# Two more x slots in a three-stage convolution network, with the second stage emitted from a table

## The chip, the cores and the metric

The kernel runs on one core of one Trainium2 chip. The metric is the device time of one execution in microseconds. The engines are TensorE (PE), VectorE (DVE), ScalarE (ACT), GpSimd (POOL), and SyncE (SP), which here only issues transfers. "Turn" means one round of the second stage's loop, one tile.

## The reference

The input x has 8192 samples of 8 channels of 16 by 16 pixels. Four layers follow each other, each of the form `x = x + layer(group_norm(x))`, with four groups of two channels:

```
x = x + tensor_train(gn(x), core0, core1, core2) + bias      # layer 0, a dense map of each sample
x = x + relu(batch_norm(conv3x3(gn(x), w1) + b1))            # layer 1, batch norm over all samples
x = x + conv3x3(quantize(gn(x)), quantize(w2)) + b2          # layer 2, int8 scale from max|gn(x)|
x = x + conv3x3(edge_pad(gn(x)), binarize(w3)) + b3          # layer 3
```

Two of these need the whole batch before they can go on. Batch norm in layer 1 needs the mean and variance over all samples, and layer 2 needs the largest absolute value of the normalised x. They cut the kernel into three stages.

## The kernel before

A tile is 128 samples: 128 partitions (channel and row) by 2048 fp32 numbers (sample and column), 1 MiB. There are 64 tiles. All stages run through them.

**Stage one** computes layer 0 and the convolution of layer 1 in quarters of a tile. It stores each tile's x (`x1_d`) and convolution output y (`y_d`) to DRAM, except those of the last four tiles, which stay in SBUF (`STAY`). A part of each quarter's input goes out to DRAM (`limb_d`) and comes back in another layout by a transfer that POOL issues (`fetch`, 252 of them, the only ones POOL issues[...]). All other large transfers are issued by SP, in order. `conv1_stats` collects mean and variance of each tile in `bnst`. At the end, a short chain over all 64 tiles turns `bnst` into the batch norm's factor and offset, `bn_a` and `bn_b`.

**Stage two** takes the tiles in `order2`, the four that stayed first. For each tile i it does, on the engine in brackets:

- load y and x (`load2`, SP), each into a slot of a ring, `y_slots` (eight) and `x_slots` (`KEEP`, 13);
- relu of y with `bn_a`, `bn_b` (ACT), then x = x + y (POOL; for a few tiles half on DVE, table `SPLIT`);
- the square of x (ACT), sums of x and its square over the groups (PE), reduction and transposition of these (DVE), two small copies (ACT), the variance (DVE), its power of -1/2 (POOL);
- the statistics widened (ACT) and spread to the samples (PE), x minus its mean (`centre2`, DVE; for three late tiles half on POOL), the store of x (SP), and the largest absolute value by sample (`range2`, DVE), combined by four tiles (`top`).

The loop's iteration i handles the add of tile i, the sums of tile i-2 and the centring of tile i-3. `InOrder` keeps the program order of PE, DVE, ACT and POOL, so the order in which the loop emits the steps is the order in which each engine does them. Of the 64 tiles, 13 stay in SBUF for stage three and are not stored (`kept`). The last five (`LATE`) load y and x into y buffers that earlier tiles have left, and are stored.

**Stage three** does layers 2 and 3 and stores the result. Its order is written out as a table of phases (`PHASE`, `PERIOD`), sorted by due time. It begins when the last `amax` is known.

Of the kernel before, what the change touches and what calls it, by code (L numbers as in the profile page):

```python
# [8 lines left out]
F32 = mybir.dt.float32  # L9
# [4 lines left out]
ALU = mybir.AluOpType  # L14
# [4 lines left out]
P = 128  # L19
# [3 lines left out]
G = 4  # L23
# [6 lines left out]
KEEP = 13  # L30
# [23 lines left out]
SPLIT = {0: 0.5, 1: 0.5, 2: 0.5, 3: 0.5, -2: 0.5, -1: 0.5}  # L54
# [9 lines left out]
def tile_net(ctx: ExitStack, tc: tile.TileContext, xb, xt_in, pack0, pack1, pack2, out):  # L64
# [22 lines left out]
    xs, bs, ys, sqs, (xh,) = ([hold.tile([P, F], F32, name=f"{n}{k}") for k in range(m)]  # L87
                            for n, m in (("xs", 4), ("bs", 2), ("ys", 2), ("sq", 2), ("xh", 1)))
# [7 lines left out]
    x_slots = ([xs[t % 4] for t in order2[:STAY]] + [u[:, h * F:(h + 1) * F] for u in us for h in range(2)] + y_stay[:3])  # L96
# [3 lines left out]
    LATE = 5 if NT >= KEEP + STAY + 3 else 0  # L100
# [19 lines left out]
    mhalf = const.tile([P, 64], F32, name="mhalf")  # L120
# [169 lines left out]
    bnst = const.tile([P, NT, 2], F32, name="bnst")  # L290
    gnst = const.tile([P, NT, 2 * G], F32, name="gnst")
# [36 lines left out]
    with first as s:  # L328
# [274 lines left out]
        for n in range(NT * NQ):  # L603
# [59 lines left out]
            if n == NT * NQ - 2 and NT > STAY + 3:  # L663
                load2(STAY)
                load2(STAY + 1)

        t = NT - 1
        if NT > STAY + 3:
            load2(STAY + 2, "x")
            load2(STAY + 3, "x")  # L670
# [5 lines left out]
        if NT > STAY + 3:  # L676
            load2(STAY + 2, "y")
# [6 lines left out]
        for i in ((t - 1, 2), (t - 1, 3), (t, 0), (t, 1), (t, 2), (t, 3)):  # L684
            conv1_stats(*i)

# [3 lines left out]
    with tc.tile_pool(name="bn", bufs=1) as bn, tc.tile_pool(name="bnp", bufs=1, space=PSUM) as bnp:  # L690
        msum = bn.tile([P, 1], F32, name="msum")
        nc.vector.tensor_reduce(msum, bnst[:, :, 0], AX.X, ALU.add)
        mps_ = bnp.tile([P, 1], F32, name="mps_")
        nc.tensor.matmul(mps_, L["avg16"], msum, start=True, stop=True)
        bmean = bn.tile([P, 1], F32, name="bmean")
        nc.vector.tensor_copy(bmean, mps_)
        dev = bn.tile([P, NT], F32, name="dev")
        nc.vector.tensor_scalar(dev, bnst[:, :, 0], bmean, None, ALU.subtract)
        nc.vector.tensor_tensor(dev, dev, dev, ALU.mult)
        nc.vector.tensor_tensor(dev, dev, bnst[:, :, 1], ALU.add)  # L700
        vsum = bn.tile([P, 1], F32, name="vsum")
        nc.vector.tensor_reduce(vsum, dev, AX.X, ALU.add)
        vps = bnp.tile([P, 1], F32, name="vps")
        nc.tensor.matmul(vps, L["avg16"], vsum, start=True, stop=True)
        bvar = bn.tile([P, 1], F32, name="bvar")
        nc.vector.tensor_scalar(bvar, vps, EPS, None, ALU.add)
        nc.gpsimd.tensor_tensor(bvar, bvar, mhalf[:, 0:1], ALU.pow)
        nc.vector.tensor_tensor(bn_a, L["gamma"], bvar, ALU.mult)
        nc.vector.tensor_tensor(bmean, bmean, bn_a, ALU.mult)
        nc.vector.tensor_tensor(bn_b, L["beta"], bmean, ALU.subtract)  # L710
# [14 lines left out]
    def stats_pow(mv):  # L725
        pool.tensor_tensor(mv[:, G:2 * G], mv[:, G:2 * G], mhalf[:, :G], ALU.pow)
# [4 lines left out]
    with tc.tile_pool(name="p2", bufs=2) as p2, tc.tile_pool(name="ps2", bufs=2, space=PSUM) as ps2:  # L731
        T = T2
        x_slots[STAY + 4:STAY + 4] = [more.tile([P, F], F32, name=f"xk{k}") for k in range(2)]
# [24 lines left out]
        def sum2(i):  # L758
            x, y = T[i]["x"], T[i].pop("y")
            y_used[i] = y  # L760
            act.activation(y, y, AF.Relu, bias=bn_b, scale=bn_a)
            n = int(F * SPLIT.get(i if i < NT // 2 else i - NT, 0))
            if n < F:
                pool.tensor_tensor(x[:, n:], x[:, n:], y[:, n:], ALU.add)
            if n:
                dve.tensor_tensor(x[:, :n], x[:, :n], y[:, :n], ALU.add)
# [9 lines left out]
        def stats2(i):  # L776

            st, mv = psc[:, 32 + 32 * (i % 2):64 + 32 * (i % 2)], gnst[:, place[order2[i]]]
            red = small.tile([P, 32], F32, name=f"s_c{i}", tag="s")
            dve.tensor_reduce(red, T[i].pop("ps").rearrange("p (b w) -> p b w", w=4), AX.X, ALU.add)  # L780
            dve.transpose(st, red)
            T[i]["sq"] = small.tile([P, G], F32, name=f"sq_c{i}", tag="sqm")
            act.copy(mv[:, 0:G], st[:, 0:G])
            act.activation(T[i]["sq"], st[:, 0:G], AF.Square)

        def sigma2(i):
            st, mv = psc[:, 32 + 32 * (i % 2):64 + 32 * (i % 2)], gnst[:, place[order2[i]]]
            dve.scalar_tensor_tensor(mv[:, G:2 * G], st[:, G:2 * G], EPS, T[i].pop("sq"), ALU.add, ALU.subtract)
            stats_pow(mv)

        def spread2(i):
            T[i]["gb"] = ps = ps2.tile([P, BANK], F32, name=f"gb_{i}", tag="gb")
            wide = p2.tile([P, 2 * G, P // G], F32, name=f"wide_{i}", tag="wide")
            act.copy(wide, gnst[:, place[order2[i]]].unsqueeze(2).to_broadcast([P, 2 * G, P // G]))
            if i % 4 == 0:
                T[i]["gr"] = ps2.tile([P, 4, P], F32, name=f"gr_{i}", tag="gr")
                T[i]["top"] = p2.tile([P, 4, P], F32, name=f"top_{i}", tag="top")
            else:
                T[i]["gr"], T[i]["top"] = T[i - 1]["gr"], T[i - 1]["top"]
            for k, dst in enumerate((ps[:, 0:P], T[i]["gr"][:, i % 4])):  # L800
                pe.matmul(dst, wide[:, k * G:(k + 1) * G].rearrange("p g n -> p (g n)"), ident, start=True, stop=True)

        def centre2(i):
            x, ps = T[i]["x"], T[i]["gb"]
            engines = [dve, dve]
            if NT - 4 <= i < NT - 1:
                engines, mean = [dve, pool], small.tile([P, P], F32, name=f"gm_{i}", tag="rows")
                a, b = HALVES[1]
                act.copy(mean[:, a:b], ps[:, a:b])
            for engine, (a, b) in zip(engines, HALVES):  # L810
                engine.tensor_tensor(samples(x)[:, a:b], samples(x)[:, a:b], over_w(ps if engine is dve else mean, a, b),
                                     ALU.subtract)
            if NT - KEEP - LATE <= i < NT - LATE:
                kept[order2[i]] = x
            else:
                nc.sync.dma_start(x2_d[order2[i]], x)
# [12 lines left out]
        def on(i, f):
            if 0 <= i < NT:  # L830
                f(i)

        BEGUN = STAY + 3 if NT > STAY + 3 else STAY
        AHEAD2 = len(y_slots) - 1


        free = STAY + AHEAD2 - 1
        for i in [*range(STAY), *range(BEGUN, free)]:
            on(i, lambda i: load2(i, "y" if i == BEGUN > STAY else "yx"))
        y_used = {}  # L840
        late = [(k, j) for j in range(NT - LATE, NT) for k in "yx"]
        for i in range(NT + 4):
            if i == 1:
                on(free, load2)
            if i + AHEAD2 < NT - LATE:
                on(i + AHEAD2, lambda i: i <= free or load2(i))
            elif late:
                k, j = late.pop(0)
                T2[j][k] = y_used[i - 1]
                nc.sync.dma_start(T2[j][k], (x1_d if k == "x" else y_d)[order2[j]])  # L850
            if i == 8:
                operands3()
            on(i, sum2)
            on(i - 2, sums2)
            on(i - 3, spread2)
            on(i - 1, square2)
            on(i - 2, stats2)
            on(i - 3, centre2)
            on(i - 2, sigma2)
            on(i - 3, range2)  # L860
# [20 lines left out]
    with ExitStack() as s:  # L881
# [4 lines left out]
        AHEAD = min(NT, KEEP - 6)  # L886
# [250 lines left out]
```

## Time and profile before

| what | value |
|---|---|
| median of 3 runs | 3813.59 us (3813.19 to 3816.85) |
| profiled execution | 3814.16 us, span 3812.4 us |
| busy share of PE, DVE, ACT, POOL | 94%, 87%, 67%, 79% |
| moved by DMA | 961.45 MB, 252 GB/s over the span |
| first relu of stage two | at 2625.65 us |
| last `top` of stage two | ends at 3059.25 us |

Shares of busy time are means over stages with different limits, so the table alone says little. Times in the text are microseconds from the start of the span. A line of a window table has the stretch, its length, then busy time and number of instructions of PE, PE's weight loads, DVE, ACT and POOL, then the granted clock of PE, the busy share of DMA, and GB/s. A line of the chain or a timeline has start, duration, engine and what is done; a bracket gives the idle time before and what ended it. A line of waits has the sum, the number and the longest.

### The profile page before, as it was taken

To read this page: it belongs to the slowest core of one execution; us is meant where nothing else is said; L and a number is where in the kernel's file an instruction comes from. 1 tells how busy PE (TensorE), PEld (TensorE's weight loads), DVE (VectorE), ACT (ScalarE), POOL (GpSimd) and SP (SyncE) were. 2 spreads that over 40 slices of the span, in tenths; PEclk is the share of its full clock that TensorE was granted. 3 is DMA by queue.
4 is the path that set the end of the run, shared out by engine and by line. 5 is a ranking of instruction groups with operands and counts; after the bars stand their busy time and mean duration, and the time that the engine had idled before them with its cause. 6 is when DMAs were issued, how large, how long until landed. Compare 5 with 4: busy or idle time off the path is not lost.

```text
span 3812.4 us, 60771 instructions
## 1 busy us (share of the span) xinstructions
PE 3585.7 (94%) x20358; PEld 2259.7 (59%) x20422; DVE 3324.4 (87%) x5896; ACT 2544.5 (67%) x2805; POOL 3006.3 (79%) x3100
## 2 busy tenths in 40 slices
PE   8999999999999999999999999997555679999999
PEld 4666666666666666666666666664444546666665
DVE  8988888888888888888888888877977888888887
ACT  5666666666666666666666666665765678888885
POOL 4877777778777777777787777765977769999998
PEclk9999999999999999999999999998866689999999
DMA  5787887887877878878878788766999824444442
GB/s 213 253 268 257 259 269 256 260 264 251 271 254 260 271 254 262 270 254 261 264 251 272 253 260 271 254 193 257 425 425 425 335 89 185 188 179 189 187 166 111
DMA packets 210840, 961.45 MB, mean 252 GB/s; under 512 B 44896, under 2 KB 45152, under 8 KB 110048
## 3 DMA queue, kind: packets, MB, share of 16 engines
q1 hardware_dynamic: 173808, 692.22, 48.9%
q0 software_dynamic: 36288, 264.26, 23.4%
q8 instruction: 163, 2.67, 0.3%
q14 instruction: 149, 1.22, 0.1%
q10 hardware_dynamic: 432, 1.08, 0.1%
HBM read 578.84 MB, written 378.54 MB: 251 GB/s over the span
## 4 chain that ended last, share of the span: by engine, by line
PE 85%; DMA 7%; POOL 4%; DVE 3%; issue 1%; ACT 1%; SPq 0%; DVEq 0%; POOLq 0%
PE po L43 45%; PE pu L43 12%; PE pf L43 10%; PE pm L43 6%; PE pq L43 4%; PE pc L43 3%; PE s L43 3%; DMA yk<-y_d 2%; POOL u L43 1%; DMA x_d<-u 1%; DMA u<-x_d 1%; POOL xs L43 1%; PE ps_a L43 1%; POOL gnst L43 1%; DMA x_d<-xk 1%
## 5 line engine op out<-in xcount | busy, mean ns | idle before, releaser
L43 PE MATMUL po<-u,core 128*128 128x512 f32 (+1 forms) x4112 | 1844.3, 591 | 0.7 <-DVE xs L43 0.7
L43 ACT COPY u<-pu 128x2048 f32<-128x2048 f32 x512 | 956.4, 1868 | 515.7 <-PE pu L43 515.6
L43 PEld LDWEIGHTS po<-u,core 128*128 128x128 f32 x4112 | 744.7, 190 | 737.4 <-issue 735.3
L43 PE MATMUL pu<-core2r,xl 128*128 128x256 f32 x4032 | 678.5, 310 | 4.8 <-ACT u L43 3.4
L43 PEld LDWEIGHTS pu<-core2r,xl 128*128 128x128 f32 x4032 | 527.9, 189 | 128.0 <-issue 123.1
L43 POOL TENSOR_TENSOR bs<-bs,xh 128x512 fp32r<-128x512 f32 (+1 forms) x253 | 325.7, 1288 | 203.6 <-ACT xh L43 201.7
L43 POOL TENSOR_TENSOR v<-e 128x128 f32<-128x128 f32 x750 | 397.3, 541 | 0.0
L43 DVE TENSOR_TENSOR xs<-po,xs 128x512 f32<-128x512 f32 x256 | 176.9, 691 | 220.3 <-PE po L43 220.3
L43 ACT ACTIVATE m<-pm,b 128x128 f32<-128x128 f32 x250 | 91.9, 368 | 394.8 <-PE pm L43 394.7
L43 PEld LDWEIGHTS pm<-v,fast 128*128 128x128 f32 x2000 | 262.5, 191 | 119.7 <-issue 105.9
L43 POOL TENSOR_TENSOR e<-x1n,x 128x512 f32<-128x512 f32 x250 | 305.5, 1222 | 31.3 <-ACT x L43 23.8
L43 DVE TENSOR_TENSOR bs<-bs,stat 128x1024 f32<-128x1024 f32 x252 | 290.5, 1214 | 2.1
L43 POOL TENSOR_TENSOR xs<-xs,w 128x2048 f32<-128x2048 f32 x64 | 291.5, 4555 | 0.7 <-DMA xs<-in_xt 0.7
L43 PE MATMUL pm<-v,fast 128*128 128x128 f32 x2000 | 263.5, 275 | 0.0
L43 ACT ACTIVATE x<-x1n 128x512 f32<-128x512 f32 x500 | 246.9, 544 | 7.6 <-DVE x1n L43 7.6
L43 PE MATMUL pf<-hi,sign 128*128 128x512 f32 x768 | 231.6, 439 | 0.4 <-ACT bs L43 0.4
L43 PE MATMUL pf<-lo,sign 128*128 128x512 f32 x768 | 218.9, 422 | 0.0
L43 POOL TENSOR_TENSOR v<-r 128x128 f32<-128x128 f32 x500 | 215.6, 447 | 0.0
L43 POOL DMA_DIRECT2D xl<-limb_d x252 | 149.8, 595 | 81.2 <-DMA limb_d<-xh 24.1
L43 POOL TENSOR_TENSOR mvb<-mvb,mhalf 128x4 f32<-128x4 f32 x64 | 66.3, 1036 | 172.0 <-DVE mvb L43 165.8
L43 PE MATMUL gb<-ident,wide 128*128 128x128 f32 x128 | 43.2, 433 | 166.6 <-ACT wide L43 166.6
L43 ACT ACTIVATE sq<-xs 128x2048 f32<-128x2048 f32 x103 | 197.4, 1917 | 1.9 <-POOL xs L43 1.7
(323 smaller groups left out, 7307.9 us busy)
## 6 DMA issues: line engine op xcount, KB each, us to landing
xl<-limb_d POOLq DMA_DIRECT2D x252, 1024.0 KB, 7.4
x_d<-xs SPq DMA_DIRECT2D x76, 1024.0 KB, 8.4
xs<-in_xt SPq DMA_DIRECT2D x64, 1024.0 KB, 7.5
bs<-in_xb SPq DMA_DIRECT2D x63, 1024.0 KB, 5.8
limb_d<-xh SPq DMA_DIRECT2D x1008, 64.0 KB, 4.5
limb_d<-bs SPq DMA_DIRECT2D x1008, 64.0 KB, 5.1
y_d<-ys SPq DMA_DIRECT2D x60, 1024.0 KB, 8.1
u<-x_d SPq DMA_DIRECT2D x34, 1024.0 KB, 6.1
```

The costliest lines, as they stand in the source:

```text
L43: return self.tc.keep_in_program_order(op(*args, **kwargs))
```

## The change

Two more x buffers (`ex`) stand in the ring of stage two, so `KEEP` is 15[...]. `LATE` becomes 6. Four x tiles rather than two are loaded around the end of stage one in another order. The batch norm is computed with a shift: the mean of 62 tiles is taken first, the sums of squares about it over 63 tiles are made before the last tile's statistics, and the last tile is added by a second matmul into the same accumulator. The second stage's steps are emitted from a table (`PHASE2`, one turn is `TURN` = 6.0), with changed times for the last five tiles (`SHIFT2`) and changed shares of DVE and POOL for the last tiles (`SPLIT`, `POOL2`). The preparation of stage three's operands (`operands3`) moves from turn 8 to turn 32.

```diff
-KEEP = 13
+KEEP = 15
...
-SPLIT = {0: 0.5, 1: 0.5, 2: 0.5, 3: 0.5, -2: 0.5, -1: 0.5}
+TURN = 6.0
+PHASE2 = {"relu": 0.0, "add": 0.3, "sums": 12.6, "rows": 18.9, "spr": 19.2, "sq": 7.5, "red": 13.8, "cp": 14.1, "cen": 20.4,
+          "store": 20.7, "sig": 15.0, "pow": 15.3, "rng": 21.6, "top": 21.9, "addv": 0.31}
+SHIFT2 = {-5: {"top": 9.4, "relu": -3, "sq": -1.3},
+          -4: {"top": 18.3, "rng": 10.2, "cen": 1.4, "store": 11.7},
+          -3: {"store": 4.0, "sums": -0.3, "cen": 3, "top": 33.8, "rng": 6.4, "sq": -4.0},
+          -2: {"sums": -3.7, "spr": 1.0, "store": 8.4, "relu": -8.6, "rng": 12.1, "sq": -3.0, "top": 46.0, "red": -2.6},
+          -1: {"cp": 0.1, "addv": 2.0, "red": 0.3, "pow": 1.3, "top": 60.5, "rng": 58.5, "store": 39.9, "spr": 10.6,
+            "cen": 16.3, "relu": -4.3, "sq": -1.0}}
+SPLIT = {0: 0.5, 1: 0.5, 2: 0.5, 3: 0.5, -2: 0.25, -1: 0.75, -3: 0.25}
+POOL2 = {-4: 0.5, -3: 0.5, -2: 0.5, -1: 0.5, -5: 0.25}
...
-    x_slots = ([xs[t % 4] for t in order2[:STAY]] + [u[:, h * F:(h + 1) * F] for u in us for h in range(2)] + y_stay[:3])
+    x_slots = ([xs[t % 4] for t in order2[:STAY]] + ex + [u[:, h * F:(h + 1) * F] for u in us for h in range(2)] + y_stay[:3])
-    LATE = 5 if NT >= KEEP + STAY + 3 else 0
+    LATE = 6 if NT >= KEEP + STAY + 3 else 0
...
-            if n == NT * NQ - 2 and NT > STAY + 3:
-                load2(STAY)
-                load2(STAY + 1)
+            for i, k in {NT * NQ - 6: [(0, "x"), (1, "x")], NT * NQ - 2: [(0, "y"), (2, "x"), (1, "y"), (3, "x")]}.get(n, []):
+                load2(STAY + i, k)
...
-            load2(STAY + 2, "x")
-            load2(STAY + 3, "x")
+        dve.tensor_reduce(shift, bnst[:, 0:seen, 0], AX.X, ALU.add)
+        load2(STAY + 4, "x")
+        load2(STAY + 5, "x")
...
-        for i in ((t - 1, 2), (t - 1, 3), (t, 0), (t, 1), (t, 2), (t, 3)):
+        mps = ps_m.tile([P, BANK], F32, name="mps", tag="mm")
+        pe.matmul(mps[:, 0:1], L["avg16"], shift, start=True, stop=True)
+        for i in ((t - 1, 2), (t - 1, 3), (t, 0), (t, 1), (t, 2)):
             conv1_stats(*i)
+        dve.tensor_scalar(shift, mps[:, 0:1], 1.0 * NT / seen, None, ALU.mult)
+        dev = small.tile([P, 2, t], F32, name="dev", tag="turned")
+        dve.tensor_scalar(dev[:, 0], bnst[:, 0:t, 0], shift, None, ALU.subtract)
+        dve.tensor_tensor(dev[:, 1], dev[:, 0], dev[:, 0], ALU.mult)
+        dve.tensor_tensor(dev[:, 1], dev[:, 1], bnst[:, 0:t, 1], ALU.add)
+        dve.tensor_reduce(part, dev, AX.X, ALU.add)
+        conv1_stats(t, 3)
+        dve.tensor_scalar(last[:, 0:1], bnst[:, t, 0:1], shift, None, ALU.subtract)
+        dve.scalar_tensor_tensor(last[:, 1:2], last[:, 0:1], last[:, 0:1], bnst[:, t, 1:2], ALU.mult, ALU.add)
...
+        for k, src in enumerate((part, last)):
+            nc.tensor.matmul(moments, L["avg16"], src, start=(k == 0), stop=(k == 1))
+        nc.vector.tensor_scalar(bvar[:, 1:2], moments[:, 0:1], moments[:, 0:1], None, ALU.mult)
+        nc.vector.scalar_tensor_tensor(bvar[:, 0:1], moments[:, 1:2], EPS, bvar[:, 1:2], ALU.add, ALU.subtract)
+        nc.gpsimd.tensor_tensor(bvar[:, 0:1], bvar[:, 0:1], mhalf[:, 0:1], ALU.pow)
+        nc.vector.tensor_scalar(nmean, moments[:, 0:1], shift, -1.0, ALU.add, ALU.mult)
+        nc.vector.tensor_tensor(bn_a, L["gamma"], bvar[:, 0:1], ALU.mult)
+        nc.vector.scalar_tensor_tensor(bn_b, nmean, bn_a, L["beta"], ALU.mult, ALU.add)
...
+            n = P - int(P * share(POOL2, i))
+            if n < P:
+                mean = small.tile([P, P], F32, name=f"gm_{i}", tag="rows")
+                act.copy(mean[:, n:], ps[:, n:P])
+                pool.tensor_tensor(x[:, n:], x[:, n:], over_w(mean, n, P), ALU.subtract)
...
+        for i, k in [(3, "y"), (6, "x"), (4, "y"), (7, "x"), (5, "y"), (6, "y")]:
+            load2(STAY + i, k)
+        todo2 = [(when(op, i), OPS2[op], (i,)) for i in range(NT) for op in OPS2]
+        todo2 += [(when("relu", i - AHEAD2, -.2), load2, (i, "y")) for i in range(STAY + AHEAD2, NT - LATE)]
+        todo2 += [(when("add", i - TURNX, .6) if i < KEEP else when("relu", i - 8, -.1), load2, (i, "x"))
+                  for i in range(TURNX, NT - LATE)]
+        todo2 += [(when("add", NT - LATE - AHEAD2 - 1 + n, .6), late2, (n,)) for n in range(2 * LATE)]
+        todo2.append((when("relu", NT // 2, -.3), operands3, ()))
...
-        AHEAD = min(NT, KEEP - 6)
+        AHEAD = min(NT, KEEP - 8)
...
-    nc = bacc.Bacc("TRN2", target_bir_lowering=False, num_devices=1)
+    nc = bacc.Bacc("TRN2", target_bir_lowering=False, num_devices=1, dynamic_dma_scratch_size=1536)
```

More of the change, by code (lines that the diff above doesn't have):

```diff
@@ L86, in tile_net @@
     hold = ctx.enter_context(tc.tile_pool(name="hold", bufs=1))
-    xs, bs, ys, sqs, (xh,) = ([hold.tile([P, F], F32, name=f"{n}{k}") for k in range(m)]
-                            for n, m in (("xs", 4), ("bs", 2), ("ys", 2), ("sq", 2), ("xh", 1)))
+    xs, bs, ys, sqs, (xh,), ex = ([hold.tile([P, F], F32, name=f"{n}{k}") for k in range(m)]
+                            for n, m in (("xs", 4), ("bs", 2), ("ys", 2), ("sq", 2), ("xh", 1), ("ex", 2)))
     us = [hold.tile([P, 2 * F], F32, name=f"u{k}") for k in range(2)]
@@ L119, in tile_net @@
     make_identity(nc, ident)
-    mhalf = const.tile([P, 64], F32, name="mhalf")
+    mhalf = const.tile([P, G], F32, name="mhalf")
     pool.memset(mhalf, -0.5)
@@ L290, in tile_net @@
     bnst = const.tile([P, NT, 2], F32, name="bnst")
+    bnw = const.tile([P, 6], F32, name="bnw")
     gnst = const.tile([P, NT, 2 * G], F32, name="gnst")
@@ L662, in tile_net @@
                 conv1(*quarter_of(n, LAG))
-            if n == NT * NQ - 2 and NT > STAY + 3:
-                load2(STAY)
-                load2(STAY + 1)
+            for i, k in {NT * NQ - 6: [(0, "x"), (1, "x")], NT * NQ - 2: [(0, "y"), (2, "x"), (1, "y"), (3, "x")]}.get(n, []):
+                load2(STAY + i, k)
         t = NT - 1
-        if NT > STAY + 3:
-            load2(STAY + 2, "x")
-            load2(STAY + 3, "x")
+        seen = max(1, NT - 2)
+        shift, nmean, part, last = bnw[:, 0:1], bnw[:, 1:2], bnw[:, 2:4], bnw[:, 4:6]
+        dve.tensor_reduce(shift, bnst[:, 0:seen, 0], AX.X, ALU.add)
+        load2(STAY + 4, "x")
+        load2(STAY + 5, "x")
         conv1_output(t - 1, 1)
@@ L675, in tile_net @@
         quarter_apply(t, 2)
-        if NT > STAY + 3:
-            load2(STAY + 2, "y")
+        load2(STAY + 2, "y")
         conv1_direct(t, 1)
@@ L690, in tile_net @@
     with tc.tile_pool(name="bn", bufs=1) as bn, tc.tile_pool(name="bnp", bufs=1, space=PSUM) as bnp:
[L691 to L710, printed above, removed]
+        moments = bnp.tile([P, 2], F32, name="moments")
+        for k, src in enumerate((part, last)):
+            nc.tensor.matmul(moments, L["avg16"], src, start=(k == 0), stop=(k == 1))
+        bvar = bn.tile([P, 2], F32, name="bvar")
+        nc.vector.tensor_scalar(bvar[:, 1:2], moments[:, 0:1], moments[:, 0:1], None, ALU.mult)
[4 more added lines that the diff above has]
+        nc.vector.scalar_tensor_tensor(bn_b, nmean, bn_a, L["beta"], ALU.mult, ALU.add)
     def sums_pe(ps, x, sq):
@@ L732, in tile_net @@
         T = T2
-        x_slots[STAY + 4:STAY + 4] = [more.tile([P, F], F32, name=f"xk{k}") for k in range(2)]
+        x_slots[STAY + 6:STAY + 6] = [more.tile([P, F], F32, name=f"xk{k}") for k in range(2)]
         y_slots += [p2.tile([P, F], F32, name=f"yk{k}", bufs=1) for k in range(4)]
@@ L756, in operands3, with relu2, share, add2 @@
             L["select"]("back2", [3], L["band3"][:, 0])
-        def sum2(i):
-            x, y = T[i]["x"], T[i].pop("y")
-            y_used[i] = y
+        def relu2(i):
+            y = T[i]["y"]
             act.activation(y, y, AF.Relu, bias=bn_b, scale=bn_a)
-            n = int(F * SPLIT.get(i if i < NT // 2 else i - NT, 0))
+        def share(table, i):
+            return table.get(i if i < NT // 2 else i - NT, 0)
+        def add2(i):
+            n = int(F * share(SPLIT, i))
             if n < F:
-                pool.tensor_tensor(x[:, n:], x[:, n:], y[:, n:], ALU.add)
+                pool.tensor_tensor(T[i]["x"][:, n:], T[i]["x"][:, n:], T[i]["y"][:, n:], ALU.add)
+        def addv2(i):
+            n = int(F * share(SPLIT, i))
             if n:
-                dve.tensor_tensor(x[:, :n], x[:, :n], y[:, :n], ALU.add)
+                dve.tensor_tensor(T[i]["x"][:, :n], T[i]["x"][:, :n], T[i]["y"][:, :n], ALU.add)
         def square2(i):
@@ L776, in stats2 @@
         def stats2(i):
-            st, mv = psc[:, 32 + 32 * (i % 2):64 + 32 * (i % 2)], gnst[:, place[order2[i]]]
+            st = psc[:, 32 + 32 * (i % 2):64 + 32 * (i % 2)]
             red = small.tile([P, 32], F32, name=f"s_c{i}", tag="s")
@@ L781, in stats2, with means2 @@
             dve.transpose(st, red)
+        def means2(i):
+            st, mv = psc[:, 32 + 32 * (i % 2):64 + 32 * (i % 2)], gnst[:, place[order2[i]]]
             T[i]["sq"] = small.tile([P, G], F32, name=f"sq_c{i}", tag="sqm")
@@ L788, in sigma2, with power2, wide2 @@
             dve.scalar_tensor_tensor(mv[:, G:2 * G], st[:, G:2 * G], EPS, T[i].pop("sq"), ALU.add, ALU.subtract)
-            stats_pow(mv)
+        def power2(i):
+            stats_pow(gnst[:, place[order2[i]]])
+        def wide2(i):
+            T[i]["wide"] = p2.tile([P, 2 * G, P // G], F32, name=f"wide_{i}", tag="wide")
+            act.copy(T[i]["wide"], gnst[:, place[order2[i]]].unsqueeze(2).to_broadcast([P, 2 * G, P // G]))
         def spread2(i):
+            wide = T[i].pop("wide")
             T[i]["gb"] = ps = ps2.tile([P, BANK], F32, name=f"gb_{i}", tag="gb")
-            wide = p2.tile([P, 2 * G, P // G], F32, name=f"wide_{i}", tag="wide")
-            act.copy(wide, gnst[:, place[order2[i]]].unsqueeze(2).to_broadcast([P, 2 * G, P // G]))
             if i % 4 == 0:
@@ L803, in centre2, with store2 @@
         def centre2(i):
[L804 to L812, printed above, removed]
+            x, ps = samples(T[i]["x"]), T[i]["gb"]
+            n = P - int(P * share(POOL2, i))
[3 more added lines that the diff above has]
+                pool.tensor_tensor(x[:, n:], x[:, n:], over_w(mean, n, P), ALU.subtract)
+            for a in range(0, n, P // 2):
+                b = min(n, a + P // 2)
+                dve.tensor_tensor(x[:, a:b], x[:, a:b], over_w(ps, a, b), ALU.subtract)
+        def store2(i):
             if NT - KEEP - LATE <= i < NT - LATE:
-                kept[order2[i]] = x
+                kept[order2[i]] = T[i]["x"]
             else:
-                nc.sync.dma_start(x2_d[order2[i]], x)
+                nc.sync.dma_start(x2_d[order2[i]], T[i]["x"])
         def range2(i):
@@ L823, in range2, with top2 @@
                                   apply_absolute_value=True)
+        def top2(i):
+            top = T[i]["top"]
             if i % 4 == 3 or i == NT - 2:
@@ L827, in range2 @@
                 dve.tensor_reduce(amax[:, at:at + 1], top[:, a:b].rearrange("p a b -> p (a b)"), AX.X, ALU.max)
[L829 to L860, printed above, removed]
+        def late2(n):
+            k, j = "yx"[n % 2], NT - LATE + n // 2
+            T2[j][k] = T[NT - LATE - AHEAD2 - 1 + n]["y"]
+            nc.sync.dma_start(T2[j][k], (x1_d if k == "x" else y_d)[order2[j]])
@@ new lines, in when @@
+        def when(op, i, more=0.0):
+            return TURN * i + PHASE2[op] + SHIFT2.get(i - NT, {}).get(op, 0) + more
+        AHEAD2, TURNX = len(y_slots) - 1, KEEP - 3
+        for i in range(STAY):
+            load2(i)
+        for i, k in [(3, "y"), (6, "x"), (4, "y"), (7, "x"), (5, "y"), (6, "y")]:
+            load2(STAY + i, k)
+        OPS2 = {"relu": relu2, "add": add2, "addv": addv2, "sums": sums2, "rows": wide2, "spr": spread2, "sq": square2,
+                "red": stats2, "cp": means2, "cen": centre2, "store": store2, "sig": sigma2, "pow": power2, "rng": range2,
+                "top": top2}
@@ L862, in tile_net @@
+        for _, f, args in sorted(todo2, key=lambda e: e[0]):
+            f(*args)
     sx = const.tile([P, 1], F32, name="sx")
```

## The prediction

> **What bounds the kernel now.** I read the slices of the page first. PE is full up to slice 27 and again from slice 33. The two lines below are DMA busy tenths and GB/s in those 40 slices of 95.3 us:
>
> ```profile
> DMA  5787887887877878878878788766999824444442
> GB/s 213 253 268 257 259 269 256 260 264 251 271 254 260 271 254 262 270 254 261 264 251 272 253 260 271 254 193 257 425 425 425 335 89 185 188 179 189 187 166 111
> ```
>
> 425 GB/s stands in slices 28 to 30 alone: this is the second stage (2626 to 3059 us), and a 1 MiB transfer (1.0486 MB) takes 1.0486/425 = 2.47 us there. The change rebuilds this stage. A table of windows shows its parts (DVE, ACT, POOL busy us, then clock, DMA share, GB/s):
>
> ```profile
> 2612.50:2623.00 10.50, 7.58 (x19) 3.20 (x17) 5.62 (x13) 2.19 (x4) 0.00 (x0) 0.95 0.05 8
> 2640.50:2645.50 5.00, 3.09 (x75) 2.32 (x77) 4.96 (x8) 4.62 (x6) 4.42 (x3) 1.00 0.38 147
> 2645.50:2654.00 8.50, 5.96 (x133) 4.73 (x132) 8.43 (x13) 7.31 (x9) 8.50 (x3) 0.80 1.01 333
> 2735.00:2990.00 255.00, 150.91 (x2486) 121.85 (x2476) 197.72 (x274) 154.88 (x180) 199.93 (x73) 0.68 1.01 425
> 3010.10:3059.30 49.20, 28.32 (x416) 22.93 (x416) 45.69 (x62) 23.79 (x35) 31.05 (x16) 0.64 0.52 210
> ```
>
> The transfers idle around the stage boundary, are full for 255 us while no engine is, and then DVE is busy 45.7 of 49.2 us. The chain of waits says the same of the middle, DMA after DMA, 20 us each because eight are in flight:
>
> ```profile
> 2797.69 19.94 DMA yk<-y_d
> 2817.70 19.90 DMA x_d<-bs
> 2837.66 19.92 DMA bs<-x_d
> ```
>
> POOL's timeline gives the two paces. Its adds (one tile each) start 5.52 us apart where POOL is the limit (add 4.57 + power 1.02, overlapping slightly) and 7.5 us apart (three transfers) where DMA is. The change of pace is seen at tile 28 (2782.8), and back at tile 56:
>
> ```profile
> 2790.33 4.56 POOL L43 TENSOR_TENSOR xs<-xs,sq 128x2048 f32<-128x2048 f32 x1 [1.96 <-ACT wide L43]
> ...
> 2993.56 4.57 POOL L43 TENSOR_TENSOR u<-u,yk 128x2048 f32<-128x2048 f32 x1 [2.05 <-DMA u<-x_d]
> ...
> 2999.08 4.59 POOL L43 TENSOR_TENSOR u<-u,yk 128x2048 f32<-128x2048 f32 x1
> ```
>
> SP's timeline shows why the transfers start late. Between the load of x of tile 10 and the first store of stage two nothing is issued for 12 us:
>
> ```profile
> 2631.22 0.32 SPq L112 DMA_DIRECT2D ys<-x_d  x1
> 2643.16 0.32 SPq L816 DMA_DIRECT2D x_d<-xs  x1
> ```
>
> [...] a DVE half add took 2.94 us beside POOL's add, 1.21 us alone.
>
> **The change, part by part.** Sums are against the profiled execution (3814.16 us, 0.57 above the median of 3813.59).
>
> *Head.* Fourteen loads (x and y of tiles 4 to 10) precede the first store now. Then two x go into the new slots before the end of stage one, so x of tiles 4 to 9 and y of 4 to 6, nine transfers instead of seven, are in by 2612, where idle time follows. From the boundary y7, x10, y8, x11, y9, y10 follow, then x12, x13, x14 as POOL frees the first tiles' y buffers (adds end about 2631, 2638, 2643): eighteen transfers precede the first store. Before, 14 had landed by 2642.5 and 17.2 by 2654 (the two windows). After, I start the stream at 2623.7 (y7 about 0.8 later than now, see batch norm) and run it without gap: 9 + (2654 - 2623.7)/2.48 = 21.2. Turns 3 to 6 then issue two transfers each per about 5.3 us against 4.95 us of transfer time, so gaps of about 0.7 us: a lead of 3.7 transfers. From both sides: 0, if the stream waits as now, to 4.5.
>
> *Middle.* In both kernels a turn issues one y, one x, one store. Count transfers from y of tile 4. Before, y of tile j is number 3j-17 and x 3j-16; after, x comes a turn earlier (3j-18), and y is 3j-16. The relu (2.09) follows y and the add follows the relu, so a tile starts one transfer later in the count: the lead is worth (3.7 - 1) x 2.48 = 6.7 us. With 15 tiles kept rather than 13 and six late ones rather than five, stores end with tile 42 (turn 45) instead of 45 (turn 48), so POOL's pace returns at tile 53 instead of 56: 3 x (7.5 - 5.52) = 5.9 us. Sum at tile 56 and, at POOL's pace, at tile 59: **12.6 us** earlier; its add starts near 2997.5 instead of 3010.1. The six late y and x come one a turn and wait only for the y buffers that adds 50 to 61 free; with 3.8 us from issue to landing, as the late stores show now, x of tile 63 is in before its add. Two reloads fewer in stage three give nothing: DMA moves 171 to 189 GB/s there.
>
> *Batch norm.* Now 5.3 us pass from the last output statistics (2620.4) to the first relu (2625.65). After: the mean's matmul sits behind the last convolution matmul on PE, five small DVE steps (0.16 to 0.25 each, 1.1 us with gaps) must fit before the last tile's statistics, which therefore end 0.8 later; then two steps, one accumulated matmul (0.54), two steps, POOL's power 0.55, two steps: relu near 2624.6, 1.0 us earlier. Behind the mean's wait on DVE stand the last statistics, and SP's y7 waits for those. Since DMA sets tile 53, only its start counts; 0.8 is already in the stream's start. No gain of its own; bounds -1 to +1.
>
> *Operands of stage three.* Moved from turn 8 to turn 32. Its DVE work runs 2667.6 to 2672.0 and opens a 3.9 us hole in POOL at tile 9. Both places are worth nothing: the DMA limit covers the hole before, and at turn 32 DVE has 2 us idle a turn and eight transfers in flight stand ahead of any late store. Without that cover it is 4 us.
>
> *Tail.* From add 59 to the last top now: 49.2 us, DVE 45.7. DVE loses half of centre 63 (-1.2) and a quarter of centre 59 (-0.5), and gets 0.25 + 0.25 + 0.75 of three adds for 0.5 + 0.5 of two (+0.7). Laying the table's order on the engines with the rows' durations, the end comes 46.5 us after add 59 if POOL and DVE adds never collide, 51 us if each 0.25 add of DVE waits out POOL's 3.5 us. Moving tops and ranges behind the centre steps hides the gaps (3.9 us on POOL before power 62). I take 47.5: **1.7 us** gained, bounds -2 to +3. POOL takes four half centres (1.93 each) in gaps; powers and adds queue behind them, which is in the two layouts. SP's six late stores end after DVE, with DMA at half load: nothing.
>
> *Nothing elsewhere.* Merging loops into a table leaves the middle's order within a turn the same. Two loads go out 45 us before stage one's end, where no input load is left to collide with. If POOL's fetch issue stays at 0.6 us, stage one is PE's (2581.6 of 2600 us).
>
> Sum: 12.6 + 1.7 = 14.3 of the profiled 3814.16, so 3799.9; in the median 3799.3, rounded to **3800**.
>
> **Rivals.** (1) *The early loads wait as before* (lead 0): SP runs in order, and y8 behind x10 waits for memory that batch norm held (the wait of 3.3 us at xk now). For it: SP's waits at 2621 and 2625. Against: 12 us of idle queue follow. Then 5.9 - 2.5 + 1.7 = 5.1: 3808.5. (2) *Better tail and full lead*: 4.5 x 2.48 - 2.5 + 5.9 + 3 = 17.6: 3796, or 3793 if DVE's waits for POOL vanish as well. (3) *Slower: the small reserve stalls POOL in stage one.* [...] Per quarter (10.1 us) POOL is busy 7.7 and issues for 0.6, so 1.9 us are spare; beyond that each us per fetch costs 252 us. [...] Against: a fetch lands in 7.4 us, before the next is issued. (4) *The table's tail costs what the head gives*, or the slots aren't used: 3810 to 3814.
>
> **How the numbers follow.** The likeliest case has 0.64 (its own range 3796 to 3806: lead +-1 transfer, tail -2 to +3), rival 1 0.14, rival 2 0.11, rival 3 0.06, rival 4 0.05. The range 3790 to 3811 takes in all but rival 3, part of rival 4 and the ends of the others, near 0.15. About 0.2% (7.6 us) is what a measurement can tell. Faster: 0.62 + 0.11 + 0.05 of rival 1 = 0.78; slower 0.06; the rest, 0.16, the same.
>
> **What would show it.** Right: four x loads more before the first store near 2643; no GB/s below 400 from 2624 on; three transfers a turn until the add of tile 52 and 5.5 us from tile 53; add 59 near 2997; the last top near 3045; stage one's end and stage three's length unchanged. Wrong: a hole in SP's timeline after x11; fetch issues over 1 us; a tail over 51 us; the first relu later than 2625.7.

## The result, and the profile after

The changed kernel takes **3805.6 us** (median of 12, 3802.71 to 3812.64), the kernel before 3814.59 us in runs beside it (median of 12). The ratio is 0.9978, 95% interval 0.9969 to 0.9987: 9.0 us faster. The prediction was 3800.0 in a range of 3790 to 3811. The profiled execution took 3807.01 us, its span is 3805.2 us, 7.2 us shorter than before's.

The same two rows of the page's slices, DMA busy tenths and GB/s:

```profile
DMA  6787887887877878888878878766999724444432
GB/s 224 252 279 253 262 267 259 259 269 252 265 260 252 272 254 262 269 251 265 268 255 261 266 252 270 255 207 248 422 423 423 320 79 189 188 180 187 187 144 111
```

The full slices are still 28 to 30; slice 31, where the stage leaves the DMA limit, is emptier (320 against 335). The table of windows, with the stage's tail cut anew from add 59 to the last `top`:

```profile
2612.50:2623.00 10.50, 8.23 (x23) 3.73 (x21) 6.80 (x17) 2.75 (x4) 0.00 (x0) 1.00 0.06 27
2640.50:2645.50 5.00, 4.49 (x78) 3.67 (x79) 4.96 (x8) 4.61 (x6) 4.39 (x3) 0.68 1.02 418
2645.50:2654.00 8.50, 5.76 (x124) 4.81 (x122) 8.41 (x13) 7.29 (x9) 8.50 (x3) 0.80 0.99 387
2735.00:2960.00 225.00, 132.60 (x2171) 108.18 (x2163) 175.23 (x250) 138.29 (x161) 176.62 (x65) 0.70 1.01 423
2999.70:3049.90 50.20, 24.61 (x416) 19.82 (x416) 47.58 (x62) 24.11 (x37) 33.03 (x18) 0.69 0.56 219
```

Where before moved 147 GB/s ahead of the first store, 418 GB/s stand now. The middle is as it was. The tail has DVE busy for 47.6 us instead of 45.7. The chain of waits in the middle is still made of transfers of 20 us:

```profile
2788.04 20.61 DMA xs<-x_d
...
2808.71 19.62 DMA bs<-y_d
...
2835.79 19.90 DMA x_d<-ys
```

SP's timeline, where before had a hole of 12 us: x of tiles 12 to 14 (the second and third line) fill it.

```profile
2626.60 0.97 SPq L125 DMA_DIRECT2D yk<-y_d  x2
2631.14 3.63 SPq L125 DMA_DIRECT2D ys<-x_d  x2
2638.56 0.32 SPq L125 DMA_DIRECT2D bs<-x_d  x1
2643.07 0.32 SPq L848 DMA_DIRECT2D x_d<-xs  x1
```

POOL's timeline at the second change of pace. The lines are the adds of tiles 52, 53, 54 and 59:

```profile
2958.96 4.56 POOL L43 TENSOR_TENSOR u<-u,sq 128x2048 f32<-128x2048 f32 x1 [1.97 <-ACT sq L43]
...
2966.49 4.57 POOL L43 TENSOR_TENSOR u<-u,sq 128x2048 f32<-128x2048 f32 x1 [2.00 <-ACT sq L43]
...
2971.98 4.62 POOL L43 TENSOR_TENSOR u<-u,xh 128x2048 f32<-128x2048 f32 x1
...
2999.69 4.64 POOL L43 TENSOR_TENSOR sq<-sq,sq 128x2048 f32<-128x2048 f32 x1
```

7.53 us from 52 to 53, then 5.49: POOL's pace is back at tile 53, as predicted. Set against before, the differences of the profiled executions add up:

| point | before | after | gained since the point above |
|---|---|---|---|
| add 53 | 2971.06 | 2966.49 | 4.6 |
| add 59 | 3010.10 | 2999.69 | 5.8 |
| end of the last `top` | 3059.25 | 3049.92 | -1.1 |
| first quantised output of stage three (`v`) | 3062.42 | 3054.76 | -1.7 |
| end of the span | 3812.4 | 3805.2 | -0.5 |

The head and the earlier end of the stores give 10.4 us. The tail and the hand-over to stage three give 2.7 of them back. The size of the tail's loss is less sure than the table looks: from add 59 to the last `top` the changed kernel's profile has 50.2 us, and five profiles of runs below that have the same tail have 48.0 to 49.9; with before's tail three profiles have 48.7 to 49.1. The loss is seen where DVE and POOL share the adds of tiles 61 and 62, first in DVE's timeline, then in POOL's:

```profile
3012.18 3.44 DVE L43 TENSOR_TENSOR yk<-yk,yk 128x512 f32<-128x512 f32 x1
3020.72 2.90 DVE L43 TENSOR_TENSOR sq<-sq,yk 128x512 f32<-128x512 f32 x1
```

```profile
3011.60 3.47 POOL L43 TENSOR_TENSOR yk<-yk,yk 128x1536 f32<-128x1536 f32 x1 [0.41 <-ACT yk L43]
3018.63 1.02 POOL L43 TENSOR_TENSOR gnst<-gnst,mhalf 128x4 f32<-128x4 f32 x1 [3.56 <-DVE gnst L43]
3019.62 3.45 POOL L43 TENSOR_TENSOR sq<-sq,yk 128x1536 f32<-128x1536 f32 x1
```

A DVE centring of 512 columns takes 0.68 us in the same tail. The adds of that size took 3.44 and 2.90 us, and each ended 0.55 us after POOL's. What stood behind them on DVE was late, and POOL then stood idle for 3.56 us for a variance that DVE owed it.

### The profile page after: what moved, and what is told of

It is laid out like the page before. It is cut to its first block, busy times and chain, and to the rows that moved or that the text cites. A ratio compares the mean times of both kernels' runs of the same rounds, so it can differ in the third digit from the quotient of the medians.

```text
span 3805.2 us, 60843 instructions
## 1 busy us (share of the span) xinstructions
PE 3587.9 (94%) x20424; PEld 2259.4 (59%) x20424; DVE 3327.7 (87%) x5899; ACT 2543.4 (67%) x2807; POOL 3006.9 (79%) x3102
## 3 DMA queue, kind: packets, MB, share of 16 engines
q1 hardware_dynamic: 173232, 688.03, 49.1%
## 5 line engine op out<-in xcount | busy, mean ns | idle before, releaser
L43 PE MATMUL pq<-q,band 128*128 128x480 bf16 (+1 forms) x768 | 189.5, 383 | 7.6 <-ACT q L43 7.6
```

What stands on the lines that cost most here:

```text
L43: return self.tc.keep_in_program_order(op(*args, **kwargs))
```

## The experiments

Each was run beside the kernel before (3814.1 to 3814.6 us in all of them). Medians are compared with the changed kernel's 3805.6. "After the first relu" takes out that stage one ended up to 2 us earlier or later from one profile to the next.

**Head: the loads of x 12 to 14 a few turns later.**

```diff
-        todo2 += [(when("add", i - TURNX, .6) if i < KEEP else when("relu", i - 8, -.1), load2, (i, "x"))
+        todo2 += [(when("relu", i - 8, -.1), load2, (i, "x"))
```

> x of tiles 12, 13 and 14 are loaded one a turn from turn 4 on, with one load a turn moved behind the first store, instead of before it. Theory (the head's early transfers set the DMA-bound middle): 15 transfers instead of 18 precede the first store, DMA idles some 6 us before 2645, the count at 2660 falls by 2.6 transfers, and every add from tile 30 to tile 59 comes 6 us later: 3811 to 3812 us. Rival (the early loads are hidden anyway, the gain comes from fewer stores and the table): 3805 to 3806 us, adds in place.

Measured: 3811.84 us (ratio 0.9993, 0.9985 to 1.0001), 6.2 more than the changed kernel. Add 59 starts 379.8 us after the first relu instead of 374.1 (before: 384.5). The windows from 2580 to 2660, first of the kernel before, then the changed kernel, then this one, show the bytes:

```profile
2580.00:2660.00 80.00, 62.71 (x547) 39.21 (x545) 61.54 (x136) 43.95 (x50) 42.50 (x34) 0.87 0.60 233
```

```profile
2580.00:2660.00 80.00, 64.17 (x550) 40.34 (x548) 62.88 (x139) 43.94 (x50) 43.16 (x35) 0.87 0.63 249
```

```profile
2580.00:2660.00 80.00, 61.55 (x544) 38.58 (x543) 62.90 (x140) 44.36 (x52) 43.60 (x34) 0.89 0.58 227
```

249 against 227 GB/s over 80 us is 1.76 MB or 1.7 transfers; 5.7 us of add 59 at 2.48 us each would be 2.3. In this run stage one ended 1.3 us earlier, so the windows do not cover the same work: begun 45 us before each run's own first relu, they hold 252 and 224 GB/s, 2.1 transfers apart. These three loads are worth all that the head gives, and a little more: add 53 starts 340.9 us after the first relu in the changed kernel, 346.6 here, and 345.4 in before.

**Stores: tiles 43 to 45 stored again, while still kept**, so that three more stores pass before the DMA limit ends.

```diff
                 kept[order2[i]] = T[i]["x"]
+                if i < NT - KEEP - LATE + 3:
+                    nc.sync.dma_start(x2_d[order2[i]], T[i]["x"])
```

> The first three kept tiles (43, 44, 45) are stored as well, and still kept; nothing reads these three stores. Theory: turns 46 to 48 have three transfers again, POOL's pace of 5.5 us returns at tile 56 instead of 53, and add 59 comes 3 x (7.5 - 5.5) = 6 us later: 3811 to 3812 us. Rival (the end of the DMA-bound stretch is set by the loads, not by the stores): under 2 us, 3805 to 3807 us.

Measured: 3811.07 us (0.9991, 0.9984 to 0.9997), 5.5 more. POOL's timeline of this run, adds of tiles 53 to 57; its own pace comes back only at 56, where before had it:

```profile
2967.43 4.55 POOL L43 TENSOR_TENSOR u<-u,sq 128x2048 f32<-128x2048 f32 x1 [1.99 <-ACT sq L43]
...
2974.96 4.57 POOL L43 TENSOR_TENSOR u<-u,xh 128x2048 f32<-128x2048 f32 x1 [2.00 <-ACT xh L43]
...
2982.59 4.56 POOL L43 TENSOR_TENSOR xk<-xk,yk 128x2048 f32<-128x2048 f32 x1 [2.09 <-ACT yk L43]
...
2990.08 4.57 POOL L43 TENSOR_TENSOR xk<-xk,yk 128x2048 f32<-128x2048 f32 x1 [1.95 <-ACT yk L43]
...
2995.59 4.59 POOL L43 TENSOR_TENSOR ys<-ys,yk 128x2048 f32<-128x2048 f32 x1
```

**Tail: before's order and shares in the changed kernel.**

```diff
-SHIFT2 = {-5: {"top": 9.4, "relu": -3, "sq": -1.3},
...
-SPLIT = {0: 0.5, 1: 0.5, 2: 0.5, 3: 0.5, -2: 0.25, -1: 0.75, -3: 0.25}
-POOL2 = {-4: 0.5, -3: 0.5, -2: 0.5, -1: 0.5, -5: 0.25}
+SHIFT2 = {}
+SPLIT = {0: 0.5, 1: 0.5, 2: 0.5, 3: 0.5, -2: 0.5, -1: 0.5}
+POOL2 = {-4: 0.5, -3: 0.5, -2: 0.5}
```

> The changed times and shares of the last five tiles are put back to what they were before (no SHIFT2; DVE has half the adds of tiles 62 and 63; POOL half the centres of 60 to 62). Theory (the new tail gives nothing, DVE's adds wait for POOL's): from add 59 to the last top 49 us instead of 50.2: 3804 to 3806 us. Rival (the new tail is a part of the gain): 3808 to 3812 us.

Measured: 3803.98 us (0.9971, 0.996 to 0.9983), 1.6 less than the changed kernel. From add 59 to the last `top` it is 48.7 us instead of 50.2, and the hand-over is 1.2 us shorter. The new tail brings nothing as it stands, and seems to cost something: the two intervals overlap, but each of the seven runs (3801.35 to 3804.74) lies below eleven of the changed kernel's twelve.

**Reserve: before with `dynamic_dma_scratch_size=1536`**, the setting of the changed kernel that the prediction and the expectation call the reserve.

```diff
-    nc = bacc.Bacc("TRN2", target_bir_lowering=False, num_devices=1)
+    nc = bacc.Bacc("TRN2", target_bir_lowering=False, num_devices=1, dynamic_dma_scratch_size=1536)
```

> The kernel before with the descriptor reserve of 1536 bytes and nothing else. Theory: the fetch issue stays at 0.6 us and nothing moves: 3813 to 3816 us. Rival (a small reserve makes POOL wait): issues over 1 us, stage one and the whole longer by 252 us for each us over the 1.9 us to spare.

Measured: 3815.04 us (1.0, 0.9992 to 1.0008). The groups of the page show the fetch's issue at 596 ns (595 in both others):

```profile
L43 POOL DMA_DIRECT2D xl<-limb_d x252 | 150.1, 596 | 90.6 <-DMA limb_d<-xh 27.6
```

The setting costs nothing here, and rival 3 is excluded. Whether the two slots need the setting is in no trace.

**No quarter adds for tiles 61 and 62.**

```diff
-SPLIT = {0: 0.5, 1: 0.5, 2: 0.5, 3: 0.5, -2: 0.25, -1: 0.75, -3: 0.25}
+SPLIT = {0: 0.5, 1: 0.5, 2: 0.5, 3: 0.5, -1: 0.75}
```

> The changed kernel with the quarter adds of the tiles 61 and 62 taken off the VectorE again (SPLIT keeps only the last tile's 0.75): GpSimd adds both tiles whole, 4.6 us each instead of 3.47 and 3.45. Theory 'the engines block each other': the two VectorE adds took 3.44 and 2.90 us beside GpSimd's adds for some 0.65 us of work, so GpSimd's longer add ends only some 0.6 us later than the VectorE's did for tile 61, the centring of tile 59 no longer stands behind it, sigma and power of tile 60 come 2 to 3 us earlier, and add 62 begins near 3017 instead of 3019.4: the end of the last top 1.5 to 2.5 us earlier, median 3803 to 3804. Rival 'sharing the adds helps': the two tiles end 1.1 us each later and the kernel is 1 to 2 us longer, 3807.

Measured: 3801.38 us (0.9966, 0.9954 to 0.9979), 4.2 less, where 1.6 to 2.6 were expected. POOL does more work and DVE 6.1 us less in a tail that is 4.1 us shorter (the window from add 59 to the last `top`):

```profile
2996.90:3043.00 46.10, 25.07 (x416) 20.68 (x416) 41.46 (x60) 24.02 (x37) 35.18 (x18) 0.69 0.64 243
```

These adds are the tail's lost time: the seven profiles with them have tails of 48.0 to 50.5 us, the two without them 46.1 and 45.5. In the changed kernel's trace DVE's two adds took 3.44 and 2.90 us and ended 0.55 us after POOL's adds of 3.47 and 3.45 us, for some 0.65 us of work (an estimate, between half of the 1.21 us that DVE's add of 1024 columns took in before without POOL's add beside it, and the 0.68 us of the centring of 512 columns). What holds DVE in that time is in no trace. While POOL adds, giving DVE a quarter of the add saves POOL 1.1 us (4.56 and 4.54 us for the whole add here) and costs DVE almost the whole of POOL's time.

**The last tile's centring on DVE alone.**

```diff
-POOL2 = {-4: 0.5, -3: 0.5, -2: 0.5, -1: 0.5, -5: 0.25}
+POOL2 = {-4: 0.5, -3: 0.5, -2: 0.5, -5: 0.25}
```

> The changed kernel with the last tile's centring on the VectorE alone (POOL2 without -1). In the changed kernel the all-reduce of the maximum began 1.4 us after its input was there and 5.9 us after GpSimd's last instruction before it, in before and in the run with the old tail 0.14 us after its input and 7.4 to 7.5 us after that instruction. Theory 'the all-reduce comes no sooner than 5.6 us after GpSimd's previous instruction': here GpSimd's last instruction is near 3040.8, the all-reduce begins within 0.2 us of its input, the VectorE's 1.2 us more of centring and the 1.3 us less of waiting cancel, median 3805 to 3806. Rival 'it waits for something else, such as stores that are landing': the wait stays near 1.4 us and the kernel is 1.2 us longer, 3806.8.

Measured: 3805.41 us (0.9975, 0.9965 to 0.9985), no difference in the median, as the theory said. The all-reduce in POOL's timeline, of before, the changed kernel, the run without quarter adds, and this run; the bracket has POOL's idle time ahead of it:

```profile
3059.71 0.38 POOL L872 PARTITION_ALL_REDUCE gm<-pm  x1 [7.53 <-DVE pm L871]
```

```profile
3051.52 0.38 POOL L899 PARTITION_ALL_REDUCE gm<-pm  x1 [5.86 <-issue]
```

```profile
3044.44 0.38 POOL L899 PARTITION_ALL_REDUCE gm<-pm  x1 [5.69 <-issue]
```

```profile
3048.55 0.38 POOL L899 PARTITION_ALL_REDUCE gm<-pm  x1 [9.34 <-DVE pm L898]
```

Where POOL's last instruction lies far enough back (7.53 and 9.34 us here), the all-reduce begins 0.14 us after its input `pm`. Where it doesn't, 1.1 to 1.6 us after `pm`, with POOL idle for 5.6 to 6.05 us and no wait in sight. So the wait is counted from POOL's last instruction, as this run shows: there that instruction ended earlier, at 3039.21, and the wait was gone. What POOL does in that time is in no record. Two MODIFY_POOL_CONFIG records of the all-reduce's line, of 12 to 13 ns each, stand at the end of POOL's preceding instruction in both kernels: at 3045.6 in the changed one, where that instruction ended at 3045.66, and at 3052.1 in before, where it ended at 3052.18. The table had put half of the last centring on POOL to save DVE 1.2 us, and so POOL's last instruction ended 4.3 us before the last `top` ended, where in before it was 7.1.

**x of tiles 10 and 11 loaded before the end of stage one**, into stage one's own buffers (`xl`), and x from tile 15 on a turn earlier.

```diff
-        xls = [const1.tile([P, F], F32R, name=f"xl{k}") for k in range(2)]
+        xls = [hold.tile([P, F], F32R, name=f"xl{k}", tag=f"xl{k}") for k in range(2)]
...
+        x_slots[STAY + 6:STAY + 6] = [hold.tile([P, F], F32, name=f"xk{k}", tag=f"xl{k}") for k in range(2)]
+        load2(STAY + 6, "x")
+        load2(STAY + 7, "x")
...
-        todo2 += [(when("add", i - TURNX, .6) if i < KEEP else when("relu", i - 8, -.1), load2, (i, "x"))
+        todo2 += [(when("add", i - TURNX, .6) if i < KEEP else when("relu", i - 9, -.1), load2, (i, "x"))
```

> The changed kernel with the two xk slots laid on the two buffers that stage one reads x into (xl), so that x 10 and x 11 can be asked for as soon as the last expansion has read them, near 2596, instead of after the batch norm at 2625; and the x loads from tile 15 on one turn earlier in SP's order (9 turns ahead instead of 8). Theory 'the length of stage two is its bytes less the lead in transfers': up to 2 more transfers done in the half idle time before 2622, each worth 2.48 us of add 59 or more, minus what the slots' reuse costs: add 59 3 to 5 us earlier, median 3801 to 3803. Rival 'the slots, not the bytes, set the pace after the head': no change, 3805.6, with the time lost again at the first stores.

Measured: 3817.2 us (1.0007, 0.9999 to 1.0015), 11.6 more, where 3801 to 3803 was expected. ScalarE's timeline has the last output of stage one and the first relu 10 us late:

```profile
2630.56 0.69 ACT L43 ACTIVATE bs<-pd,b 128x512 f32<-128x512 f32 x1 [1.89 <-PE pd L43]
2635.43 4.08 ACT L43 ACTIVATE ys<-ys,bn_b,bn_a 128x2048 f32<-128x2048 f32 x2 [4.18 <-DVE bn_b L728]
```

Stage one was 0.16 us a tile longer from the first tile on; why moving `xl` does that stays open. Stage two can still be judged. Over the 80 us that begin 45 us before the first relu, DMA moved 265 GB/s here and 252 in the changed kernel, a lead of one transfer; yet add 59 started 374.75 us after the first relu, not earlier (374.14). So here a lead in bytes was not enough. That it was x which came early, while the adds waited for relus and so for y, fits the timeline but was not tested.

**Before's batch norm in the changed kernel** (the code lines of before in their old place).

> The changed kernel with before's batch norm (all of it after the last statistics). Theory 'the first relu comes 0.7 us later, and nearly all transfers that matter are not waiting for it': median 3805.6 to 3806.3, the same as the changed kernel within what can be told. Rival 'the whole head follows the batch norm, the first stores and all after it': 0.7 to 1.0 us longer, 3806.3 to 3806.6. A difference above 2 us would say that the batch norm did more than either.

Measured: 3805.6 us (0.9977, 0.9968 to 0.9986), no difference. The idle time before the first relu is 5.43 us here; the changed kernel has 4.60:

```profile
2626.12 4.08 ACT L43 ACTIVATE ys<-ys,bn_b,bn_a 128x2048 f32<-128x2048 f32 x2 [5.43 <-DVE bn_b L723]
```

```profile
2625.55 4.08 ACT L43 ACTIVATE ys<-ys,bn_b,bn_a 128x2048 f32<-128x2048 f32 x2 [4.60 <-DVE bn_b L725]
```

**operands3 back at turn 8.**

```diff
-        todo2.append((when("relu", NT // 2, -.3), operands3, ()))
+        todo2.append((when("relu", 8, -.3), operands3, ()))
```

> The changed kernel with operands3 (the weights of stage three) back at turn 8, where before has it, instead of turn 32. In before it made one turn of 9.4 us at tile 9, where GpSimd sets the pace and the DMA queues are full; in the changed kernel one of 8.3 us at tile 32 where the usual is 7.5. Theory 'the early hole lies where the lead in transfers is still being used up, so it is mostly paid for with lead and not with time; the late one lies where every turn waits for a transfer': the 3.9 us hole at tile 9 comes back, the turn to the 7.5 us pace comes one tile later, the 0.8 us at tile 32 go: add 59 within 1 us of the changed kernel, median 3805 to 3806.5. Rival 'the hole at tile 9 was lost time and the move brought it back': add 59 some 3 to 4 us later, median 3809.

Measured: 3806.17 us (0.9979, 0.9972 to 0.9987), no difference. The hole is back in POOL's timeline (first line, ahead of the add of tile 9), and the adds of tiles 30 to 32 below it are where the pace changes now:

```profile
2674.33 1.02 POOL L43 TENSOR_TENSOR gnst<-gnst,mhalf 128x4 f32<-128x4 f32 x1 [3.87 <-DVE gnst L43]
```

```profile
2792.28 4.58 POOL L43 TENSOR_TENSOR xs<-xs,xh 128x2048 f32<-128x2048 f32 x1 [0.17 <-ACT xh L43]
...
2799.95 4.56 POOL L43 TENSOR_TENSOR xs<-xs,yk 128x2048 f32<-128x2048 f32 x1 [2.10 <-ACT yk L43]
...
2808.52 4.57 POOL L43 TENSOR_TENSOR xs<-xs,yk 128x2048 f32<-128x2048 f32 x1 [3.04 <-ACT yk L43]
```

POOL keeps its own pace two tiles longer and add 59 comes 374.00 us after the first relu: the hole is paid for with lead. One part of the expectation failed. The turn of tile 32 is 8.57 us long although operands3 is elsewhere, so the 8.3 us of the changed kernel there were not operands3 either. A turn like it stands at tile 48 in both kernels (8.25 us in the changed one, 8.32 in before). What these turns are stays open.

**A mended tail**: no quarter adds, a quarter of the last centring on POOL, the last relu ahead of the square of tile 61 on ScalarE.

```diff
-            "cen": 16.3, "relu": -4.3, "sq": -1.0}}
+            "cen": 16.3, "relu": -9.0, "sq": -1.0}}
...
-SPLIT = {0: 0.5, 1: 0.5, 2: 0.5, 3: 0.5, -2: 0.25, -1: 0.75, -3: 0.25}
-POOL2 = {-4: 0.5, -3: 0.5, -2: 0.5, -1: 0.5, -5: 0.25}
+SPLIT = {0: 0.5, 1: 0.5, 2: 0.5, 3: 0.5, -1: 0.75}
+POOL2 = {-4: 0.5, -3: 0.5, -2: 0.5, -1: 0.25, -5: 0.25}
```

> The changed kernel with three numbers of its tables changed: no quarter adds for the tiles 61 and 62, as in the run without them (3801.4); a quarter instead of half of the last tile's centring on GpSimd, so that GpSimd's last instruction ends near 0.9 us sooner and the VectorE's last top 0.6 us later; and the last tile's relu 4.7 us earlier in the order, ahead of the square of tile 61. In the run without the quarter adds that relu (2.1 us) stood on ScalarE between the row copy of tile 59 and the copy of tile 60's means, and the VectorE waited 3.1 us for what came behind it, while ScalarE itself had waited 2.4 us for GpSimd just before. Theory 'each engine's order in the tail is what costs': the relu fills ScalarE's wait, the VectorE's 3.1 us shrink to about 1.3, the all-reduce waits 0.1 to 0.7 us instead of 1.2: 1.5 to 2.5 us less, median 3799 to 3800. Rival 'the last y has not landed by then': the relu holds the square of tile 61 back, no gain, 3801 to 3803.

Measured: **3800.31 us** (0.9966, 0.9953 to 0.9978), the lowest of all: 5.3 less than the changed kernel; it is 1.1 less than without the quarter adds alone, which is within what chance can give. The all-reduce waits for its input again, with 6.10 us of idle POOL:

```profile
3045.33 0.38 POOL L899 PARTITION_ALL_REDUCE gm<-pm  x1 [6.10 <-DVE pm L898]
```

The relu helped less than expected: it began 1.3 us after ScalarE was free, when its y had landed, so the square of tile 61 was held back, and DVE's wait of 3.1 us shrank only to 2.4.

## Why the prediction was right, and where it was off

The direction, the range and the bound were right: transfers set the middle, and the change gets more of them done early and fewer in the middle. The profiled time fell by 7.2 us where the sum said 14.3; the terms:

- **Head: 6.7 predicted, 4.6 measured** (add 53). The lead is 3.2 transfers instead of 3.7: 16 GB/s more over 80 us are 1.2 transfers, and the other two, x of tiles 4 and 5, were issued long before the boundary. The line of one buffer's transfers shows it: the slots `ex` are free from the start, and SP's first two loads into them are at 67.9 and 121 us, not near 2600 as I had placed them.

```profile
L125 SPq DMA_DIRECT2D ex<-x_d x8: 319/320/437, 67.9 to 2916.0; - x8
```

  The missing half transfer lies at the start of the stream, which the prediction ran "without gap". Only y of tile 7 was issued before the batch norm's end, at 2622.70; all else stood in SP's order behind x of tile 10, which waited 2.4 us for `bn_b`. Before, two loads of y were ahead of that wait, at 2621.51. SP's timeline, first of before (one line), then of the changed kernel (two lines), and the windows of the stream's start, first of before, then of the changed kernel:

```profile
2621.51 0.80 SPq L112 DMA_DIRECT2D yk<-y_d  x2
```

```profile
2622.70 0.32 SPq L125 DMA_DIRECT2D yk<-y_d  x1
2625.29 0.32 SPq L125 DMA_DIRECT2D xk<-x_d  x1
```

```profile
2623.00:2640.50 17.50, 9.42 (x139) 7.34 (x140) 8.57 (x17) 12.87 (x10) 12.53 (x6) 0.64 1.00 414
2623.00:2640.50 17.50, 9.93 (x139) 7.61 (x140) 8.48 (x16) 12.96 (x10) 12.63 (x6) 0.60 0.96 386
```

  28 GB/s less over 17.5 us are 0.47 transfers: rival 1's mechanism, at a small size. The gap of turns 3 to 6 was as predicted, 0.7 us (387 instead of 423 GB/s over 8.5 us); the sign "no GB/s below 400" left that gap out. (3.2 - 1) x 2.48 is 5.5 us; of the 0.9 us still missing, 0.7 lie in the turn of tile 32 (8.3 us, before 7.6), which stays open.
- **Stores: 5.9 predicted, 5.8 measured**, at the tile predicted. The run with three stores more gives 5.5 us back.
- **Batch norm: 1.0 us earlier and no gain predicted; no gain measured.** From the last output of stage one to the first relu it is 0.83 us less than with before's batch norm in the same kernel, and 0.69 less than in before. The first relu itself came at 2625.55, not near 2624.6, since stage one ended 0.6 us later in this profile.
- **Operands3: nothing, and nothing measured.** The reason given for tile 9 held, the one for tile 32 can't be told.
- **Tail: 1.7 gained predicted, 1.1 lost measured.** This is the step that failed: "I take 47.5", between 46.5 without collisions and 51 with DVE's quarter adds waiting out POOL's. Measured were 50.2 with those adds (48.0 to 49.9 in other profiles of the same tail) and 46.1 without them. The high end was the nearer one, and its reason was the right one. Before's own 2.94 us for a DVE add beside POOL's, against 1.21 us for one without, said that such adds side by side do collide, so the high end was the one to lean to.
- **Hand-over: not in the sum, 1.7 lost.** I ended the tail at the last `top` and didn't ask how long POOL takes from its last centring to the all-reduce, 5.86 us in this profile. 1.1 of it is the later start of the all-reduce: it began 1.6 us after the last `top` instead of 0.5, and in the three runs in which it waits for its input again (before's tail, the last centring on DVE, the mended tail) it is 0.3. The other 0.5 stand between the all-reduce and `v` (3.2 us, before 2.7), where two small memsets now come after the reciprocal on DVE; moving them was not tried, and the other runs with this order have 2.85 to 3.3 us.
- **Stage three: unchanged predicted, 0.5 longer measured.** From `v` to the end the profiles of these kernels differ by 2.3 us without a pattern, so nothing is read into it.

The undone parts agree with the whole: 6.2 (three loads of the head) + 5.5 (stores) + 0.0 (batch norm) + 0.6 (operands3) - 1.6 (tail) = 10.7 against 9.0 us, with several us of uncertainty in each by the intervals; the run without the three loads also took out some 1.2 us more than the head had given. Emitting the steps from a table was not undone alone; what the other parts leave for it lies within that uncertainty. Of the rivals, 1 as a whole (no lead) is excluded by the lead that the windows show, and 3 by its own run, whose issues took 596 ns where the rival needed over 1 us; 2 failed with the tail. Rival 4 was part of the truth: the tail and what hangs on it took 2.7 of the 10.4 us that head and stores gave. That the mended tail comes to 3800.3, near the predicted 3800, is luck in part: the head gives 2 us less than predicted there too, and the tail is 2 us shorter than predicted (45.5 instead of 47.5).

## What to carry to other kernels

In a stage bound by transfers, count in transfers, but not at their full time of 2.48 us (1.0486 MB at 423 GB/s). The three stores taken out of the middle paid 2 us each, since POOL's own pace of 5.5 us a tile took over from 7.5. The lead of 3.2 transfers paid 4.6 us, since a tile in the new order starts one transfer later and 0.9 us were lost on the way; one transfer more of lead, in the run with x of tiles 10 and 11, paid nothing. What was done to the compute engines ahead of it and in it (batch norm, operands3) paid nothing. Where the limit changes to compute, at the tail, giving DVE a quarter of an addition while POOL adds the rest was no sharing (3.44 and 2.90 us on DVE beside 3.47 and 3.45 on POOL): price it at the longer of the two, and ask what stands behind it on the engine that waits. And price an engine's way from its last ordinary instruction to a special one, here 5.6 to 6.05 us ahead of POOL's all-reduce, as well as the instruction's own 0.38 us.

## What the runs showed of the hardware

- POOL's all-reduce came no sooner than 5.6 to 6.05 us after POOL's previous instruction in the seven profiles where its input was early; with 6.10 us or more between them it began 0.14 us after its input. It stands as "issue" in the profile (5.86 us in the changed kernel); before, with 7.53 us from POOL's previous instruction to the all-reduce, did not show it.
- The transfers do not all stand in SP's queue where the program's text asks for them: two whose buffers were free from the start were issued at 67.9 and 121 us, some 2500 us ahead.
- With `dynamic_dma_scratch_size=1536` POOL issued the 252 fetches of 1 MiB, one every 10 us, in 595 ns each in the changed kernel and 596 in before's program; without it before took 595.
